# A perceiver block on one core: attention weights scaled by the product that turns them, and a context layer norm's scale and bias on GpSimd

## The chip, the cores and the metric

The kernel runs on one core of a Trainium2 chip. The metric is the device time of one execution in microseconds; the number given is the median of several runs. A profile of one execution comes with it. Engines are named as the profile names them: PE is TensorE (PEld its loads of the stationary operand), DVE is VectorE, ACT is ScalarE, POOL is GpSimd, SP is SyncE, which issues most DMAs.

## The reference, cut to what matters

64 sequences of 32 tokens of width 256 attend to contexts of 257 rows each. Two layers follow each other; each adds a cross attention, a self attention and a feed-forward part to the tokens. The two cross attentions are what the change touches.

```python
# layer 0: keys and values from the normed context and the tokens themselves
xn = layernorm(ctx, ln_x_g, ln_x_b)          # (x - m) / sqrt(v + eps) * g + b
ln = layernorm(latents, ln_l_g, ln_l_b)
q = ln @ Wq
kv = concatenate([xn @ Wkv, ln @ Wkv])       # 257 + 32 keys, 16 heads of 64
sim = einsum(rmsnorm(q) * scale, rmsnorm(k)) # masked
out = softmax(sim) @ v;  out @ Wout + bout
...
# layer 1: keys and values from the raw context, 257 keys, 16 heads of 64
scores = (q / 8) . k;  out = softmax(scores) @ v;  out @ wo + bo
```

The other parts are a self attention with 16 heads of 16, a mixture of 64 experts (8 per token, capacity 128) with a shared expert, a causal self attention in a latent space, and a linear part with tanh.

## The kernel before, in words

All arithmetic is in float32. The 2048 tokens are 16 tiles of 128 rows, each four sequences (`NB` = 4, `b` is the place in the tile). The program has three stages: `before` (layer 0 up to the routing), `experts`, and `after` (layer 1). PE's instruction order is written by hand: the whole program stands in a manual schedule for PE. The other engines' orders come from a planner, which also decides whether a copy written as `nc.any.tensor_copy` runs on DVE or ACT; `urgent()` raises the priority of what is issued inside it.

`before` loops over the 64 sequences with `CrossFirst`. One pass `s` does, in PE's order: `keys(s+2)` (16 products that make the keys of 16 heads, copies to kT at L1230 and L1232, squares at L1235), `weigh(s)`, `norms(s+2)` (L1247, sums of those squares), `values(s)` (L232, L242), `spread(s+2)` (L1268), `turn(s+3)` (L1202, contexts transposed), `scores(s+2)` (L1287, then masking and softmax), and `prepare(s+4)` (layer norm of a context, on DVE and ACT alone). Between these, `slot()` issues a piece of the tile work of the tokens: queries of the next tile, the output projection, self attention, routing. The routing ends in a scatter by eight indirect DMAs that POOL issues per tile (L665).

Scores lie with queries (4 heads x 32 tokens, four groups `g`) on the partitions and keys along the row. `softmax_rows` takes the maximum (L193), exponentials with sums (L195), a reciprocal (L198), and then scales the rows by the reciprocal: two groups on DVE (L208), two on ACT (L206). The last 33 columns are also written scaled to a second place in the tile (`twice`, L201), which the product with the tail of the values needs. `weigh` transposes the scaled weights, three chunks of 128 keys times four groups, against an identity (`keyed`, L218), and copies them to `at` (L219). `prepare` (L1183 on) subtracts the mean and multiplies by g (L1189), then multiplies by the reciprocal deviation and adds b (L1190), on DVE for each half of 128 rows; the result `cx` is what `turn` transposes and `values` reads.

`after` does the same for layer 1 with `CrossSecond`, with raw contexts and no key matrix: pass `s` is `weigh(s)`, `scores(s+2)`, `values(s)` with slots between. Its scaling is at L1393 on DVE for all four groups, its transpositions at L1405 (the third chunk repeats the last key's column over 128 columns, by a broadcast), its copies at L1406.

A product of the program, `product` (L178), is one `nc.tensor.matmul` per pair of operands: `lhsT` is the stationary operand, `rhs` the moving one. In the profile's rows the moving operand is named first after the arrow: psT<-c,sim is a transposition with sim stationary and the identity (a slice of the constants c) moving.

Of the kernel before, what the change touches and what calls it, by code (L numbers as in the profile page):

```python
# [10 lines left out]
F32 = mybir.dt.float32  # L11
# [3 lines left out]
ALU = mybir.AluOpType  # L15
AX = mybir.AxisListType

P = 128
D = 256
S = 32  # L20
NB = P // S
J = 257
JK = J + S
# [76 lines left out]
class Kernel:  # L100
    def __init__(self, ctx, tc, a, out):
        self.ctx, self.tc, self.nc, self.a, self.out = ctx, tc, tc.nc, a, out
        self.nt = out.shape[0] // P
        self.nb = self.nt * NB
        self.const = ctx.enter_context(tc.tile_pool(name="const", bufs=1))
        self.ps = ctx.enter_context(tc.tile_pool(name="ps", bufs=8, space=bass.MemoryType.PSUM))
        self.small = ctx.enter_context(tc.tile_pool(name="small", bufs=4))
# [76 lines left out]
        nc.vector.tensor_tensor(xt, xt, ps, ALU.add)  # L184


    def softmax_rows(self, sim, n, twice=None):


        nc = self.nc  # L190
        mx = self.small.tile([P, 4], F32, name="mx")
        sm = self.small.tile([P, 4], F32, name="sm")
        nc.vector.tensor_reduce(mx, sim, AX.X, ALU.max, negate=True)  # L193
        for g in range(4):
            nc.scalar.activation(  # L195
                sim[:, g, :], sim[:, g, :], AF.Exp, bias=mx[:, g : g + 1], accum_out=sm[:, g : g + 1]
            )
        nc.vector.reciprocal(sm, sm)  # L198
        if twice is not None:
            m = twice.shape[2]  # L200
            nc.vector.tensor_tensor(  # L201
                twice, sim[:, :, n - m :], sm.unsqueeze(2).to_broadcast([P, 4, m]), ALU.mult
            )
        for g in range(4):
            if g % 2:
                nc.scalar.mul(sim[:, g, :], sim[:, g, :], sm[:, g : g + 1])  # L206
            else:
                nc.vector.tensor_scalar(sim[:, g, :], sim[:, g, :], sm[:, g : g + 1], None, ALU.mult)  # L208

    def keyed(self, sim, sizes):  # L210

        nc = self.nc
        at = self.atp.tile([P, len(sizes), 512], F32, name="at")
        k0 = 0
        for j, n in enumerate(sizes):
            ps = self.bank("psT")
            for g in range(4):
                nc.tensor.transpose(ps[:n, g * P : (g + 1) * P], sim[:, g, k0 : k0 + n], self.ident)  # L218
            nc.any.tensor_copy(at[:n, j, :], ps[:n, :])  # L219
            k0 += n  # L220
        return [at[:n, j, :] for j, n in enumerate(sizes)]
# [454 lines left out]
    def experts(self, ctx, slot, tails):  # L676
# [75 lines left out]
        for e in range(AHEAD):  # L752
            weigh(e)
# [17 lines left out]
        for e in range(E):  # L771
            weigh(e + AHEAD)
            fetch(e + 3)
            turn(e + 2)
            while (at - total + rest) * E < rest * e:
                next(side)
                at += 1
            inner(e + 1)
            outer(e)
            if e == AHEAD:  # L780
                self.after_weights()
            if e == 2 * AHEAD:
                self.ffnw = self.ffn_weights(self.w2)
# [319 lines left out]
class CrossFirst:  # L1103


    def __init__(self, k, kp):
        self.k, self.kp = k, kp
        self.own, self.held, self.cx, self.xT = {}, {}, {}, {}

    def given(self, wq, wk, gx, bx, gl, bl, gam, xl, xlT):  # L1110
        self.wq, self.wk_ = wq, wk
# [71 lines left out]
    def prepare(self, s):  # L1183

        k, nc, cx = self.k, self.k.nc, self.cx[s]
        mv, rs = k.stats(cx, 2)
        for j in range(2):
            x = cx[:, j, :]
            nc.vector.scalar_tensor_tensor(x, x, mv[:, j, 0:1], self.gx, ALU.subtract, ALU.mult)  # L1189
            nc.vector.scalar_tensor_tensor(x, x, rs[:, j : j + 1], self.bx, ALU.mult, ALU.add)  # L1190

    def turn(self, s):

# [78 lines left out]
    def scores(self, s):  # L1272
        k = self.k
        nc = k.nc
        t, b = divmod(s, NB)
        _, _, qT, mb = self.own[t]
        _, _, kT, whole = self.held[s]
        sim = whole[:, :, :JK]
        for half in range(2):
            ps = [k.bank("psB") for _ in range(2)]  # L1280
            for u in range(2):
                for i in range(2):
                    for odd in range(2):
                        m = 2 * (2 * half + i) + u
                        q = PLACES[i].index(2 * u + odd)
                        r = slice(DH * odd, DH * odd + DH)
                        nc.tensor.matmul(  # L1287
                            ps[i][q * S : (q + 1) * S, :JK],
                            lhsT=qT[r, m, b * S : (b + 1) * S],
                            rhs=kT[r, m, :],  # L1290
                            start=True,
                            stop=True,
                        )
            for i in range(2):
                g = 2 * half + i
                with k.urgent():
                    nc.vector.tensor_tensor(sim[:, g, :], ps[i][:, :JK], sim[:, g, :], ALU.mult)  # L1297
        nc.vector.tensor_tensor(sim, sim, mb[:, b, :].unsqueeze(1).to_broadcast([P, 4, JK]), ALU.add)
        k.softmax_rows(sim, JK, whole[:, :, 2 * P + 64 : 2 * P + 64 + S + 1])

    def weigh(self, s):

        k = self.k
        cx, c3, _, sim = self.held.pop(s)
        at = k.keyed(sim, [P, P, P])
        self.weights = at[:2], [cx[:, 0, :], cx[:, 1, :]], (at[2], c3)

    def values(self, s):
# [7 lines left out]
class CrossSecond:  # L1316
# [54 lines left out]
    def scores(self, s):  # L1371

        k, nc = self.k, self.k.nc
        t, b = divmod(s, NB)
        cx, xT = self.cx[s]
        qk = self.qk[t]
        sim = self.kp.tile([P, 4, J], F32, name="sim")
        mx = k.small.tile([P, 4], F32, name="mx")
        sm = k.small.tile([P, 4], F32, name="sm")
        for g in range(4):  # L1380
            ps = k.bank("psY")
            k.product(
                ps[:, :J],
                [qk[:, c, b, g * P : (g + 1) * P] for c in range(2)],
                [xT[:, c, :] for c in range(2)],
            )
            nc.vector.tensor_reduce(mx[:, g : g + 1], ps[:, :J], AX.X, ALU.max, negate=True)  # L1387
            nc.scalar.activation(  # L1388
                sim[:, g, :], ps[:, :J], AF.Exp, bias=mx[:, g : g + 1], accum_out=sm[:, g : g + 1]
            )  # L1390
        nc.vector.reciprocal(sm, sm)
        for g in range(4):
            nc.vector.tensor_scalar(sim[:, g, :], sim[:, g, :], sm[:, g : g + 1], None, ALU.mult)  # L1393
        self.held[s] = sim

    def weigh(self, s):

        k, nc = self.k, self.k.nc
        sim = self.held.pop(s)
        at = self.kp.tile([P, 3, 512], F32, name="at", bufs=1)  # L1400
        for j in range(3):
            ps = k.bank("psT")
            for g in range(4):
                x = sim[:, g, j * P : (j + 1) * P] if j < 2 else sim[:, g, J - 1 :].to_broadcast([P, P])
                nc.tensor.transpose(ps[:, g * P : (g + 1) * P], x, k.ident)  # L1405
            nc.any.tensor_copy(at[:, j, :], ps)  # L1406
        self.at = at

# [93 lines left out]
```

## Time and profile before

| what | value |
|---|---|
| median of 3 runs | 2816.75 us (2816.62 to 2820.55) |
| the profiled execution's own time | 2814.6 us |
| its span | 2812.4 us |
| granted TensorE clock, mean | 0.985 |
| busy: PE, DVE, ACT, POOL | 2650.2, 1730.6, 1227.6, 542.3 us |
| transpositions of weights: L218, L1405 | 768 and 768 |
| scalings of weights: L208, L206, L1393 | 128, 128, 256 |
| context layer norm: L1189, L1190 | 128, 128 |

A row of the groups names line, engine, operation, output and inputs, shapes and count, then busy time with the mean of one instruction, then the idle time of the engine ahead of it and who ended it. A row of the timeline gives start, duration, and a run of like instructions with their count; the durations of PE overlap, so a run's pace is read from the starts. A wait's row gives who waited for whom, the total, the number of waits and the longest.

### The profile page before, as it was taken

How to read it: one execution, taken by the hardware profiler on the slowest of the kernel's cores; microseconds unless marked ns; L12 is line 12 of the kernel's file. 1: busy time of each engine (PE TensorE's matmuls, PEld its weight loads, DVE VectorE, ACT ScalarE, POOL GpSimd, SP SyncE). 2: the span in 40 equal slices, each digit the busy share in tenths (PEclk: the TensorE clock that was granted, in tenths of full speed). 3: DMA queues.
4: the chain of work that ended last, by engine and by line, in shares of the span. 5: the costliest groups of instructions: out<-in, count | busy, mean ns of one | idle time of the engine just before them, and what ended most of it. 6: DMA issues, size and time to landing. Idle time of an engine off the chain costs nothing. (4 is left out here: it accounts for less than half of the span.)

```text
span 2812.4 us, 59421 instructions
## 1 busy us (share of the span) xinstructions
PE 2650.2 (94%) x23642; PEld 1823.7 (65%) x23642; DVE 1730.6 (62%) x4544; ACT 1227.6 (44%) x3463; POOL 542.3 (19%) x644
## 2 busy tenths in 40 slices
PE   6999999999999999999998799899999999999995
PEld 4566656665666566656665578677777777777763
DVE  6565656665666567656755433556666666666664
ACT  4555555555555555555553233333333333333331
POOL 3110122112211221122112200421222222121001
PEclk9999999999999999999998799999999999999997
DMA  7000011101100000000002587221212222221110
GB/s 263 27 16 14 18 31 33 31 18 31 32 30 18 27 26 22 18 19 19 17 5 82 182 268 229 80 71 48 61 48 58 52 55 59 50 57 47 33 33 7
DMA packets 136089, 157.05 MB, mean 56 GB/s; under 512 B 24025, under 2 KB 118980, under 8 KB 135813
## 3 DMA queue, kind: packets, MB, share of 16 engines
q1 hardware_dynamic: 114308, 119.65, 14.0%
q0 software_dynamic: 12288, 25.21, 3.4%
q10 hardware_dynamic: 9216, 8.39, 0.9%
q8 instruction: 187, 3.06, 0.5%
q14 instruction: 90, 0.73, 0.1%
HBM read 121.63 MB, written 37.75 MB: 57 GB/s over the span
## 5 line engine op out<-in xcount | busy, mean ns | idle before, releaser
L178 PE MATMUL psA<-xT,wk 128*128 128x289 f32 x2048 | 522.0, 410 | 17.9 <-issue 13.0
L178 PEld LDWEIGHTS psA<-xT,wk 128*128 128x128 f32 x2048 | 384.0, 190 | 150.1 <-issue 46.5
L802 POOL DMA_INDIRECT y<-oute,idx x128 | 131.5, 1027 | 657.4 <-DVE x L813 466.8
L232 PE MATMUL psY<-at,cx 128*128 128x512 f32 x512 | 238.1, 608 | 0.0
L178 PE MATMUL psA<-at,cx 128*128 128x512 f32 x512 | 233.5, 599 | 0.0
L178 PE MATMUL psY<-xT,qk 128*128 128x257 f32 x1024 | 233.5, 380 | 0.0
L178 PEld LDWEIGHTS psY<-xT,qk 128*128 128x128 f32 x1024 | 189.8, 190 | 25.1
L1388 ACT ACTIVATE sim<-psY,mx 128x257 f32<-128x257 f32 x256 | 120.8, 476 | 148.6 <-DVE mx L1387 147.7
L232 PEld LDWEIGHTS psY<-at,cx 128*128 128x128 f32 x512 | 92.8, 191 | 123.1 <-issue 99.7
L195 ACT ACTIVATE sim<-sim,mx 128x289 f32<-128x289 f32 x256 | 135.5, 532 | 64.4 <-DVE mx L193 64.3
L178 PEld LDWEIGHTS psA<-at,cx 128*128 128x128 f32 x512 | 93.4, 190 | 96.5 <-issue 83.3
L1235 ACT ACTIVATE sq<-kT 128x1156 f32<-128x1156 f32 x128 | 148.6, 1161 | 12.6 <-DVE kT L1232 11.4
L244 ACT COPY yT<-psY 128x512 f32<-128x512 f32 x128 | 68.7, 589 | 189.8 <-PE psY L242 189.8
L1297 DVE TENSOR_TENSOR sim<-psB,sim 128x289 f32<-128x289 f32 x256 | 100.7, 451 | 81.5 <-PE psA L178 37.9
L1230 ACT COPY kT<-psA 128x289 f32<-128x289 f32 x256 | 99.2, 388 | 115.7 <-PE psA L178 113.6
L665 POOL DMA_INDIRECT buf<-z,fi x128 | 126.4, 987 | 96.3 <-DVE fi L662 54.0
L1232 DVE COPY kT<-psA 128x289 f32<-128x289 f32 x256 | 114.3, 451 | 40.0 <-PE psA L178 39.9
L178 PE MATMUL psY<-yT,wv 128*64 128x128 f32 x2048 | 127.9, 277 | 7.3 <-DVE yT L1418 7.3
L1387 DVE TENSOR_REDUCE mx<-psY 128x1 f32<-128x257 f32 x256 | 101.0, 418 | 52.6 <-PE psY L178 47.5
L178 PEld LDWEIGHTS psY<-yT,wv 128*64 128x64 f32 x2048 | 116.6, 138 | 16.3 <-DVE yT L1418 11.2
L184 DVE TENSOR_TENSOR x<-x,psY 128x256 f32<-128x256 f32 (+1 forms) x80 | 29.2, 365 | 156.4 <-PE psY L178 154.8
L178 PE MATMUL psY<-wo,oT 128*128 128x128 f32 (+1 forms) x768 | 124.2, 315 | 0.0
(254 smaller groups left out, 5005.7 us busy)
## 6 DMA issues: line engine op xcount, KB each, us to landing
cx<-in_ctx SPq DMA_DIRECT2D x128, 256.0 KB
we<-in_m_ew SPq DMA_DIRECT2D x64, 384.0 KB
xT<-in_ctxT SPq DMA_DIRECT2D x64, 257.0 KB
buf<-zero SPq DMA_DIRECT2D x32, 256.0 KB
be<-buf SPq DMA_DIRECT2D x64, 128.0 KB
oute<-oe ACTq DMA_DIRECT2D x64, 128.0 KB
mu<-in_mask SPq DMA_DIRECT2D x16, 128.5 KB
x<-in_x SPq DMA_DIRECT2D x16, 128.0 KB
```

Source lines behind the costliest of these rows:

```text
L178: self.nc.tensor.matmul(ps, lhsT=lhs[i], rhs=rhs[i], start=(i == 0), stop=(i == n - 1))
L195: nc.scalar.activation(sim[:, g, :], sim[:, g, :], AF.Exp, bias=mx[:, g : g + 1], accum_out=sm[:, g : g + 1])
L232: nc.tensor.matmul(ps[kc], lhsT=values[i][:, kc * P : (kc + 1) * P], rhs=at[i], start=(i == 0), stop=(i == n - 1 and tail is None),)
L244: nc.any.tensor_copy(yT[:, kc, :, b * S : (b + 1) * S], ps[kc].rearrange("p (h i) -> p h i", h=H))
L665: d = nc.gpsimd.indirect_dma_start(out=self.buf[:, :], out_offset=bass.IndirectOffsetOnAxis(ap=fi[:, k : k + 1], axis=0), in_=z[:, 0, :], ...
L802: nc.gpsimd.indirect_dma_start(out=y, out_offset=None, in_=self.oute[:, :], in_offset=bass.IndirectOffsetOnAxis(ap=self.idx[:, t, k : k + ...
L1230: nc.scalar.copy(kT[:, p, :], ps[:, :JK])
L1232: nc.vector.tensor_copy(kT[:, p, :], ps[:, :JK])
L1235: nc.scalar.activation(sq[p // 4], kT[:, p - 3 : p + 1, :], AF.Square)
L1297: nc.vector.tensor_tensor(sim[:, g, :], ps[i][:, :JK], sim[:, g, :], ALU.mult)
L1387: nc.vector.tensor_reduce(mx[:, g : g + 1], ps[:, :J], AX.X, ALU.max, negate=True)
L1388: nc.scalar.activation(sim[:, g, :], ps[:, :J], AF.Exp, bias=mx[:, g : g + 1], accum_out=sm[:, g : g + 1])
```

## The change

The rows of the weights are no longer scaled. `diagonal` makes, for each group, the identity with the reciprocal sums on its diagonal (`dg`, one DVE operation for all four groups), and `turned` multiplies the unscaled weights with it instead of transposing them against the identity: the product transposes and scales at once. The copy of the last 33 columns to their second place is now unscaled and runs on GpSimd. The contexts' layer norm in `prepare` is done by `layernorm` (subtract and multiply by the reciprocal deviation, L152, on DVE), and its scale g and bias b follow on GpSimd as two operations over both halves.

```diff
-    def softmax_rows(self, sim, n, twice=None):
+    def softmax_rows(self, pool, sim, n, twice=None):
...
+        if twice is not None:
+            nc.gpsimd.tensor_copy(twice, sim[:, :, n - twice.shape[2] :])
+        return self.diagonal(pool, sm)
+
+    def diagonal(self, pool, sm):
+
+        nc = self.nc
         nc.vector.reciprocal(sm, sm)
-        if twice is not None:
-            m = twice.shape[2]
-            nc.vector.tensor_tensor(
-                twice, sim[:, :, n - m :], sm.unsqueeze(2).to_broadcast([P, 4, m]), ALU.mult
-            )
-        for g in range(4):
-            if g % 2:
-                nc.scalar.mul(sim[:, g, :], sim[:, g, :], sm[:, g : g + 1])
-            else:
-                nc.vector.tensor_scalar(sim[:, g, :], sim[:, g, :], sm[:, g : g + 1], None, ALU.mult)
+        dg = pool.tile([P, 4, P], F32, name="dg", bufs=2)
+        nc.vector.tensor_tensor(
+            dg, self.ident.unsqueeze(1).to_broadcast([P, 4, P]), sm.unsqueeze(2).to_broadcast([P, 4, P]), ALU.mult
+        )
+        return dg
+
+    def turned(self, ps, x, dg):
+
+        self.nc.tensor.matmul(ps, lhsT=x, rhs=dg, start=True, stop=True)
...
-                nc.tensor.transpose(ps[:n, g * P : (g + 1) * P], sim[:, g, k0 : k0 + n], self.ident)
+                self.turned(ps[:n, g * P : (g + 1) * P], sim[:, g, k0 : k0 + n], dg[:, g, :])
...
     def prepare(self, s):
 
         k, nc, cx = self.k, self.k.nc, self.cx[s]
-        mv, rs = k.stats(cx, 2)
-        for j in range(2):
-            x = cx[:, j, :]
-            nc.vector.scalar_tensor_tensor(x, x, mv[:, j, 0:1], self.gx, ALU.subtract, ALU.mult)
-            nc.vector.scalar_tensor_tensor(x, x, rs[:, j : j + 1], self.bx, ALU.mult, ALU.add)
+        k.layernorm(cx, cx)
+        nc.gpsimd.tensor_tensor(cx, cx, self.gx.unsqueeze(1).to_broadcast([P, 2, D]), ALU.mult)
+        nc.gpsimd.tensor_tensor(cx, cx, self.bx.unsqueeze(1).to_broadcast([P, 2, D]), ALU.add)
...
-        k.softmax_rows(sim, JK, whole[:, :, 2 * P + 64 : 2 * P + 64 + S + 1])
+        dg = k.softmax_rows(self.kp, sim, JK, whole[:, :, 2 * P + 64 : 2 * P + 64 + S + 1])
+        self.ready[s] = dg
...
-        nc.vector.reciprocal(sm, sm)
-        for g in range(4):
-            nc.vector.tensor_scalar(sim[:, g, :], sim[:, g, :], sm[:, g : g + 1], None, ALU.mult)
-        self.held[s] = sim
+        self.held[s] = sim, k.diagonal(self.kp, sm)
...
-                nc.tensor.transpose(ps[:, g * P : (g + 1) * P], x, k.ident)
+                k.turned(ps[:, g * P : (g + 1) * P], x, dg[:, g, :])
```

In the kernel after the change these lines lie at L199 (copy on GpSimd), L207 (dg), L214 (the turning product, in both stages), L225 and L1408 (copies to `at`), L1193 and L1194 (scale and bias on GpSimd).

More of the change, by code (lines that the diff above doesn't have):

```diff
@@ L197, in softmax_rows, with keyed @@
             )
-        nc.vector.reciprocal(sm, sm)
-        if twice is not None:
-            m = twice.shape[2]
-            nc.vector.tensor_tensor(
-                twice, sim[:, :, n - m :], sm.unsqueeze(2).to_broadcast([P, 4, m]), ALU.mult
-            )
-        for g in range(4):
-            if g % 2:
-                nc.scalar.mul(sim[:, g, :], sim[:, g, :], sm[:, g : g + 1])
-            else:
-                nc.vector.tensor_scalar(sim[:, g, :], sim[:, g, :], sm[:, g : g + 1], None, ALU.mult)
-    def keyed(self, sim, sizes):
+        if twice is not None:
[3 more added lines that the diff above has]
+        nc = self.nc
+        nc.vector.reciprocal(sm, sm)
+        dg = pool.tile([P, 4, P], F32, name="dg", bufs=2)
[5 more added lines that the diff above has]
+        self.nc.tensor.matmul(ps, lhsT=x, rhs=dg, start=True, stop=True)
+    def keyed(self, sim, dg, sizes):
         nc = self.nc
@@ L1107, in __init__ @@
         self.k, self.kp = k, kp
-        self.own, self.held, self.cx, self.xT = {}, {}, {}, {}
+        self.own, self.held, self.cx, self.xT, self.ready = {}, {}, {}, {}, {}
     def given(self, wq, wk, gx, bx, gl, bl, gam, xl, xlT):
@@ L1304, in weigh @@
         cx, c3, _, sim = self.held.pop(s)
-        at = k.keyed(sim, [P, P, P])
+        at = k.keyed(sim, self.ready.pop(s), [P, P, P])
         self.weights = at[:2], [cx[:, 0, :], cx[:, 1, :]], (at[2], c3)
@@ L1390, in scores @@
             )
-        nc.vector.reciprocal(sm, sm)
-        for g in range(4):
-            nc.vector.tensor_scalar(sim[:, g, :], sim[:, g, :], sm[:, g : g + 1], None, ALU.mult)
-        self.held[s] = sim
+        self.held[s] = sim, k.diagonal(self.kp, sm)
     def weigh(self, s):
         k, nc = self.k, self.k.nc
-        sim = self.held.pop(s)
+        sim, dg = self.held.pop(s)
         at = self.kp.tile([P, 3, 512], F32, name="at", bufs=1)
```

## The prediction

> **What bounds the kernel now.** I read the page's first two parts first: who is busy, and whether that holds in every stage.
>
> ```profile
> PE 2650.2 (94%) x23642; PEld 1823.7 (65%) x23642; DVE 1730.6 (62%) x4544; ACT 1227.6 (44%) x3463; POOL 542.3 (19%) x644
> ...
> PE   6999999999999999999998799899999999999995
> PEclk9999999999999999999998799999999999999997
> ```
>
> TensorE is busy 94% of the span and shows a 9 in nearly every slice, at the full granted clock; no other engine passes two thirds. A busy PE need not be PE at its limit, so I asked for the two stretches of attention (first: 64 sequences by the loop with `turn`, `keys`, `weigh`; second: 64 sequences with `CrossSecond`). Columns: length, then busy time and count of PE, PEld, DVE, ACT, POOL, granted clock, DMA.
>
> ```profile
> 60.00:1450.00 1390.00, 1347.19 (x11379) 855.22 (x11377) 893.99 (x2483) 746.75 (x2058) 272.46 (x358) 1.00 0.09 25
> 1930.00:2780.00 850.00, 818.32 (x8320) 608.97 (x8319) 554.56 (x1271) 289.98 (x862) 160.26 (x154) 1.00 0.18 49
> ```
>
> PE lacks 42.8 us of 1390 in the first and 31.7 of 850 in the second. So every microsecond added to PE's own stream there is added to the end, except where it falls into one of these gaps; and a microsecond taken from DVE or ACT buys nothing unless it shortens one. Which gaps those are is told by the waits of PE in the first stretch:
>
> ```profile
> PE psA L178 <- issue: 12.1, 28, 1.0
> PE psB L1247 <- ACT sq L1235: 10.3, 14, 2.0
> PE psB L1287 <- ACT qTf L1167: 6.7, 15, 1.8
> ```
>
> In the loop's order `norms` (L1247) comes after `weigh`, so its 10.3 us (14 waits, mean 0.74) is time that a longer `weigh` covers. L1287 waits for a copy of transposes that were issued after `weigh`; it isn't covered. The second stretch's largest wait, 14.0 us for zT (L162), lies between a transposition and its own product, nowhere near `weigh`.
>
> **The change, part 1: what a turned tile costs on PE.** The 12 transpositions of a sequence become 12 products with a scaled diagonal. The group rows say that one record of either takes the same: 275 and 273 ns (transpositions, L1405 and L218) against 278 (psA<-zT,wq, an ordinary product of the same shape). That is the time through the pipeline, not the pitch. The pitch comes from the timeline (start, duration, count), where the next row's start closes each burst:
>
> ```profile
> 2016.27 3.84 PE L178 MATMUL psA<-zT,wq 128*128 128x128 f32 x32 [0.73 <-ACT zT L162]
> 2019.95 1.47 PE L1405 MATMUL psT<-c,sim 128*128 128x128 f32 x12
> 2021.26 1.03 PE L178 MATMUL psY<-xT,qk 128*128 128x257 f32 x4
> ...
> 1651.61 1.06 PE L178 MATMUL psA<-beT,we 128*128 128x128 f32 x8
> 1652.50 0.60 PE L178 MATMUL psY<-we,eact 128*128 128x256 f32 x2
> ```
>
> The transpositions: (2021.26 - 2019.95)/12 = 109 ns each. The products: (2019.95 - 2016.27)/32 = 115 ns and (1652.50 - 1651.61)/8 = 111 ns a record. And the count is what matters: `queries` writes 16 products for zT,wq and the trace has 32 records; `inner` writes 4 and it has 8; `weigh` writes 12 transpositions and it has 12. An f32 product is two records, a transposition is one. A turned tile therefore goes from 109 ns to between 2 x 111 = 222 and 2 x 115 = 230 ns: 113 to 121 more. There are 768 in each stretch, 1536 in all: 1536 x 0.113 = 174 us to 1536 x 0.121 = 186 us. I take 1536 x 0.118 = 181 us, a little nearer the bigger row, because mixed streams (psY<-wo,oT, 116 to 118 ns in the timeline) sit there. Per sequence that is 1.41 us.
>
> A rule speaks here. The Trainium skill, "TensorE: Matmul & The Clock Gate", section Terms, says that the transposition mode is four times faster for FP32. By it a product would cost 4 x 109 = 436 ns and the change 1536 x 0.327 = 502 us, a time near 3319. The rows above contradict that as a pitch: products with 128 columns stand at 222 to 230. The same page, section LDWEIGHTS, has a load of the stationary operand last columns/1.2 ns, 107 for 128: both kinds load 128 columns per record, and that floor hides most of the fourfold. I go by the rows.
>
> **Part 2: what leaves DVE and ACT.** DVE loses the scaling of weights (256 of L1393 at 364 ns, 128 of L208 at 377, 64 of L201 at 295: 160 us) and of contexts (128 of L1189 at 476, 128 of L1190 at 544: 131 us); it gains 128 diagonals (128x512 with two inputs; nearest row L309, 683 ns: 87 us) and 128 passes of normalising (two per context; L152, 256 columns, 0.44 us: 56 us). ACT loses 128 of L206 at 536 ns (69 us). The planner that places `any` copies answers by moving copies of `at`: in the built order DVE has 63 of 384 where it had 212, so 149 x 0.68 = 101 us more leave DVE and 149 x 0.59 = 88 us come to ACT. Sum: DVE about -249, ACT about +19. On the path this is worth only what it takes from PE's waits: nothing beyond the L1247 row, which part 1 covers too. I count it once: -10 us.
>
> The new wait: `weigh` now waits for the diagonal. Behind it in PE's queue stand `norms`, `values`, `spread` and all that follows. In the timeline a sequence's last L208 ends at 664.3 and its `weigh` starts at 683.6, 19 us later; a 0.68 us diagonal in place of two scalings comes no later. Zero; without that cover it would be 0.7 x 128 = 87 us.
>
> **Part 3: what comes to GpSimd.** Two operations of 128x512 for each of 64 contexts. Bounds for one: twice L1123 (128x256, 774 ns) gives 1.5 us, twice L1122 (919) gives 1.8, L1011 (128x512, strided input) 1.53. I take 1.5: 128 x 1.5 = 192 us, and 64 copies of 4x33 at some 0.4 us (L1206, 64 elements, 0.31): 26 us. POOL goes from 542 to 760 us. No DMA moves with it, but POOL's queue carries the scatter of routed rows (8 DMA issues at 1.28 us pitch after a 4.3 us wait, some 15 us per tile) and the mask (L1174, 3.64 us). In the built order a context's two operations stand ahead of the scatter that could hold them, and the copy into the tail of the weights follows the scatter only where its `weigh` is over a sequence away. The tightest place that I find: DVE ends a context at 705.9, PE turns the next at 719.1; 3 us more of POOL fit into 13. Zero, with the bound of a full miss in the rivals. At the start POOL gets three contexts' operations, 9 us, between 18 and 35 us, before q (L1151 ended at 31.7, read by PE at 33.1): about +1 us, once.
>
> **Sum.** Against the profiled execution's own 2814.6 us (span 2812.4): 2814.6 + 181 - 10 + 1 = 2986.6. The median of the runs is 2.2 above that execution: 2988.8, rounded to 2988.
>
> **Rivals.**
> 1. *PE's gaps swallow more.* 74.5 us of gaps stand in both stretches. If the lighter DVE also closes half of them (37 us instead of 10), 2961. Against it: the unnamed waits ("issue", 12.1 us) come once per tile wherever the scatter runs, and zT's lie elsewhere.
> 2. *GpSimd becomes the bound in the first stretch.* If contexts come late behind a scatter once per tile, 12 tiles x up to 10 us add 120: 3108; if both operations lay wholly on PE's path, 60 x 3 = 180: 3168. For it: POOL is strictly in order and holds long waits; against it: the margins of 13 us and more, and 34% use after the change (470 of 1390).
> 3. *The other side: the turning product costs no more than the transposition.* Place: L214's pitch. If the diagonal product is a single record (112 against 109 ns: 1536 x 3 ns = +5 us) while ACT's relief removes the 10 us of L1247 and a few of the rest, the time is 2817 + 5 - 12 = 2810, faster. It decides below 109 + 12/1.536 = 117 ns per tile. Against it: every f32 product in the trace has two records.
> 4. *The fourfold rule holds after all*: 3319.
>
> **How the numbers follow.** My forecast, products as record pairs and no new stall: 0.80, alone within 2970 to 3005 (174 to 186 us, with nothing or 20 us swallowed). Rival 1: 0.06; rival 2: 0.09; rival 3: 0.03; rival 4: 0.02. The range 2962 to 3015 reaches to rival 1's time and to the small end of rival 2. A measurement of this kernel tells 0.2% (5.6 us) from no change. Faster 0.03, same 0.01 (a pitch near rival 3's limit), slower 0.96.
>
> **What would show it.** Right: L214 has 1536 records in each stretch and a burst of 24 takes about 2.7 us where 12 took 1.31; the first stretch's period grows by about 1.3 us per sequence and the second's by 1.4; L1251's wait for sq is gone; DVE falls to about 1480 us, POOL rises to about 760; PE's share rises to 95%. Wrong: 12 records per burst (rival 3); a PE wait at the transposition of contexts for POOL cx L1194, or at L214 for POOL L199 or DVE dg (rival 2); a burst of 5 us (rival 4).

## The result, and the profile after

The kernel after takes 2968.62 us (median of 4, 2966.16 to 2970.87) where the kernel before takes 2816.78: ratio 1.0535, 95% interval 1.0515 to 1.0556, or +152 us. The forecast was 2988 (+171), the range 2962 to 3015. The direction and the price of the product hold; the size is 19 us off, and the parts of that are below.

The page of the kernel after, first part (busy time, share, instructions), then two of its groups on PE (line, operation, names, shapes, count; busy, mean ns; idle before):

```profile
PE 2823.4 (95%) x25178; PEld 2007.2 (68%) x25178; DVE 1576.8 (53%) x3970; ACT 1275.0 (43%) x3461; POOL 741.5 (25%) x836
...
L214 PE MATMUL psT<-dg,sim 128*128 128x128 f32 x3072 | 367.8, 276 | 2.6 <-issue 2.4
L1251 PE MATMUL psB<-sq,c 128*32 128x289 f32 x1024 | 78.9, 413 | 1.2 <-ACT sq L1239 1.0
```

PE's count has risen by 25178 - 23642 = 1536: each of the 1536 turned tiles is now two records instead of one. The mean of one record is 276 ns where the transpositions had 275 and 273, so the mean tells nothing of the price. The timeline (start, duration, run) does:

```profile
2105.46 3.84 PE L178 MATMUL psA<-zT,wq 128*128 128x128 f32 x32 [0.73 <-ACT zT L162]
2109.13 2.84 PE L214 MATMUL psT<-dg,sim 128*128 128x128 f32 x24
2111.81 3.64 PE L178 MATMUL psY<-xT,qk 128*128 128x257 f32 x16
```

The 24 records hold PE for 2111.81 - 2109.13 = 2.68 us, 111.7 ns each (PE is held from a record's start to the next record's start). The same place took 1.31 us for 12 transpositions: +1.37 us per sequence.

Where in the program the time came from is read from the starts of four bursts of turned tiles: the first, the 64th (end of the first stretch), the 65th and the 128th. First the kernel before, then the kernel after:

```profile
61.99 1.47 PE L218 MATMUL psT<-c,sim 128*128 128x128 f32 x12
...
1512.38 1.47 PE L218 MATMUL psT<-c,sim 128*128 128x128 f32 x12
...
1800.32 2.77 PE L1405 MATMUL psT<-c,sim 128*128 128x128 f32 x12
...
2745.74 1.47 PE L1405 MATMUL psT<-c,sim 128*128 128x128 f32 x12
```

```profile
64.55 2.84 PE L214 MATMUL psT<-dg,sim 128*128 128x128 f32 x24
...
1581.57 2.84 PE L214 MATMUL psT<-dg,sim 128*128 128x128 f32 x24
...
1868.14 5.01 PE L214 MATMUL psT<-dg,sim 128*128 128x128 f32 x24
...
2900.73 2.84 PE L214 MATMUL psT<-dg,sim 128*128 128x128 f32 x24
```

| stage, us | before | after | difference |
|---|---|---|---|
| start to first burst | 62.0 | 64.5 | +2.6 |
| first to 64th (63 sequences) | 1450.4 | 1517.0 | +66.6 |
| 64th to 65th (rest of the first part, experts) | 287.9 | 286.6 | -1.3 |
| 65th to 128th (63 sequences) | 945.4 | 1032.6 | +87.2 |
| 128th to the end | 66.6 | 66.2 | -0.4 |

The 65th bursts take 2.77 and 5.01 us because the granted clock was 0.50 and 0.53 there, after PE had stood for some 6 us.

In the second stretch the price of the product arrives whole: 63 x 1.37 = 86 of 87 us. In the first stretch 20 us of it are missing. Adding up, for each PE group there, the time from each record's start to the next one's: the turned tiles go from 89.9 to 174.8 us (+84.9); norms (psB<-sq) from 91.0 to 71.3 (-19.7); scores (psB<-kT,qTf) from 83.3 to 92.6 (+9.3); keys and the transpositions of z lose 5.9, and what is left of the stretch 2. The norms' gain is seen in one place of the timeline, once per tile. Before, then after:

```profile
664.17 0.68 PE L1247 MATMUL psB<-sq,c 128*32 128x289 f32 x4
665.39 1.17 PE L1247 MATMUL psB<-sq,c 128*32 128x289 f32 x12 [0.54 <-ACT sq L1235]
```

```profile
690.50 1.18 PE L1251 MATMUL psB<-sq,c 128*32 128x289 f32 x16
```

Before, PE did four norms, then stood until ACT had the second half of the squares; after, all sixteen run through. `weigh` stands ahead in PE's queue and has grown by 1.37 us. But the squares came sooner, too. Their second half at these two places, before and after:

```profile
664.19 1.15 ACT L1235 ACTIVATE sq<-kT 128x1156 f32<-128x1156 f32 x1
```

```profile
687.51 1.17 ACT L1239 ACTIVATE sq<-kT 128x1156 f32<-128x1156 f32 x1
```

Counted from the start of `weigh` (661.05 and 686.01), the squares were complete after 4.3 us before and after 2.7 us now; the norms began after 3.1 us before and after 4.5 us now. Either move alone would have been enough to end the wait here. Eleven tiles have this place, and it makes 14.5 of the 19.7 us (the other long norms stand at the start of the stretch); on the mean over them the squares went from 4.4 to 2.4 us. So this pair does not show which of the two took the wait away.

### The profile page after: what moved, and what is told of

Its sections match the earlier page's. It is cut to its first block, busy times and chain, and to the rows that moved or that the text cites. A ratio compares the mean times of both kernels' runs of the same rounds, so it can differ in the third digit from the quotient of the medians.

```text
span 2966.9 us, 62129 instructions
## 1 busy us (share of the span) xinstructions
PE 2823.4 (95%) x25178; PEld 2007.2 (68%) x25178; DVE 1576.8 (53%) x3970; ACT 1275.0 (43%) x3461; POOL 741.5 (25%) x836
## 4 chain that ended last, share of the span: by engine, by line
PE 86%; DVE 6%; ACT 4%; issue 2%; DMA 2%; POOL 0%; SPq 0%; POOLq 0%; DVEq 0%; ACTq 0%
PE psA L178 34%; PE psY L178 18%; PE psT L214 12%; PE psY L238 8%; PE psB L1251 2%; PE psY L248 2%; PE psB L1291 2%; PE psA L1353 1%; PE psY L328 1%; PE psB L178 1%; PE psT L161 1%; PE psR L1272 1%; DMA cx<-in_ctx 1%; DVE st L141 1%; ACT sim L1273 1%
## 5 line engine op out<-in xcount | busy, mean ns | idle before, releaser
L178 PE MATMUL psA<-xT,wk 128*128 128x289 f32 x2048 | 526.0, 414 | 11.3 <-issue 5.3
L178 PEld LDWEIGHTS psA<-xT,wk 128*128 128x128 f32 x2048 | 389.4, 193 | 141.8 <-issue 29.5
L214 PEld LDWEIGHTS psT<-dg,sim 128*128 128x128 f32 x3072 | 363.4, 193 | 12.9 <-issue 4.3
L214 PE MATMUL psT<-dg,sim 128*128 128x128 f32 x3072 | 367.8, 276 | 2.6 <-issue 2.4
L178 PE MATMUL psA<-at,cx 128*128 128x512 f32 x512 | 233.3, 598 | 0.0
L178 PE MATMUL psY<-xT,qk 128*128 128x257 f32 x1024 | 232.9, 380 | 0.0
L178 PEld LDWEIGHTS psY<-xT,qk 128*128 128x128 f32 x1024 | 189.3, 190 | 24.9
L1408 ACT COPY at<-psT 128x512 f32<-128x512 f32 x191 | 110.4, 585 | 176.0 <-PE psT L214 118.6
L1193 POOL TENSOR_TENSOR cx<-cx,a_gx 128x512 f32<-128x512 f32 x64 | 87.9, 1373 | 368.5 <-DVE cx L152 357.5
L178 PEld LDWEIGHTS psA<-at,cx 128*128 128x128 f32 x512 | 93.4, 190 | 96.5 <-issue 74.4
```

The lines of the kernel that those rows point to most:

```text
L178: self.nc.tensor.matmul(ps, lhsT=lhs[i], rhs=rhs[i], start=(i == 0), stop=(i == n - 1))
L214: self.nc.tensor.matmul(ps, lhsT=x, rhs=dg, start=True, stop=True)
```

## Experiments

All ran on chips 1, 5 and 13, where the kernel before takes 2751 to 2754 us, not 2817. The record names no chip for the pair above; that it was another one is inferred from the time, and "the first chip" below means the one of that pair. Each experiment is compared with the kernel before on its own chip, and the expectations given as absolute times are read as differences. In which part of the program the times differ is told with the two unchanged kernels below.

**The product alone.** The kernel before, with transpositions issued as products with the identity:

```diff
...
-                nc.tensor.transpose(ps[:n, g * P : (g + 1) * P], sim[:, g, k0 : k0 + n], self.ident)
+                nc.tensor.matmul(ps[:n, g * P : (g + 1) * P], lhsT=sim[:, g, k0 : k0 + n], rhs=self.ident, start=True, stop=True)
...
-                nc.tensor.transpose(ps[:, g * P : (g + 1) * P], x, k.ident)
+                nc.tensor.matmul(ps[:, g * P : (g + 1) * P], lhsT=x, rhs=k.ident, start=True, stop=True)
```

> The kernel before with its 12 transpositions per sequence issued as ordinary f32 products against the identity; every scaling on DVE and ACT stays. Theory (the longer weigh covers the wait of norms for the squares): 1536 x (2 x 111.5 - 109) ns = +175 us, less some 18 us of waits covered, 2974 us (2966 to 2982), and the wait of L1247 for ACT falls below 2 us. Rival (the lighter DVE and ACT took that wait away): the wait stays near 10 us and the time is 2990 us or more.

Measured 2926.54 against 2751.31: ratio 1.0631 (1.0611 to 1.0652), +175 us. So the whole loss is there without any diagonal, any scaling moved or any GpSimd work: it is the price of an f32 product against a transposition. (The planner answered this edit as well: DVE makes 111 of the 384 copies to `at` here, 212 in the kernel before and 63 in the kernel after.) The theory's time (+157) is missed, although the wait of L1247 fell to 1.9 us as it said, for two reasons that the stages show against the unchanged kernel's profile: these chips have little wait at the norms to cover (next experiments), and the last stage is 8.3 us longer here (74.5 against 66.2). PE has two unnamed stops there, 2.6 and 1.8 us, and the granted clock of that stage is 0.73 against 0.78:

```profile
PE psY L322 <- issue: 2.6, 1, 2.6
...
PE psB L1050 <- issue: 1.8, 1, 1.8
```

The two stretches alone grew by 78.7 and 82.5 us.

**The relief alone.** The kernel after with the products put back to transpositions against the identity:

```diff
     def turned(self, ps, x, dg):

-        self.nc.tensor.matmul(ps, lhsT=x, rhs=dg, start=True, stop=True)
+        self.nc.tensor.transpose(ps, x, self.ident)
```

> The kernel after with the 12 products per sequence put back to transpositions against the identity; dg is still made but not used, so the division of the attention weights by their sums is left out. Theory: without the longer weigh the wait for the squares is back (8 us or more in L1251), 2810 to 2818 us, so the relief of DVE and ACT is worth next to nothing. Rival: the relief alone takes the wait away, 2798 us or less.

Measured 2759.46 (2754.18 to 2766.93) against 2751.31: ratio 1.003 (1.0013 to 1.0046). As differences the theory had -7 to +1 us and the rival -19: measured +8, past the theory's end and away from the rival. DVE's and ACT's lighter load buys nothing here. The profiled execution was the fastest (2754.18), so where the rest of the 8 us lies is not seen. The norms hold PE for 75.6 us in the first stretch, as in the unchanged kernel (75.3); with the product alone it is 69.6. So on these chips the longer `weigh` took what wait there was, and the lighter ACT did not. That is 6 us, nearly all of it near the start of the stretch. It does not carry over to the first pair, whose waits stand mostly elsewhere.

**The contexts' scale and bias alone.** The kernel before with the new `prepare`:

```diff
-        mv, rs = k.stats(cx, 2)
-        for j in range(2):
-            x = cx[:, j, :]
-            nc.vector.scalar_tensor_tensor(x, x, mv[:, j, 0:1], self.gx, ALU.subtract, ALU.mult)
-            nc.vector.scalar_tensor_tensor(x, x, rs[:, j : j + 1], self.bx, ALU.mult, ALU.add)
+        k.layernorm(cx, cx)
+        nc.gpsimd.tensor_tensor(cx, cx, self.gx.unsqueeze(1).to_broadcast([P, 2, D]), ALU.mult)
+        nc.gpsimd.tensor_tensor(cx, cx, self.bx.unsqueeze(1).to_broadcast([P, 2, D]), ALU.add)
```

> The kernel before with only the contexts' scale and bias moved to GpSimd. Theory: hidden, within 4 us of the kernel before (2816 to 2821), the start some 2 us later. Rival: GpSimd's extra work beside the scatter is what lengthens the scores (kT,qTf) by 9 us in the kernel after, then 2824 to 2828.

Measured 2764.09 against 2751.31: ratio 1.0047 (1.003 to 1.0064), +12.8 us. Theory missed, and the rival's place too: the scores hold PE as long as before (73.3 against 73.6 us). Against the unchanged kernel's profile the start is 3.0 us longer, the first stretch 7.4 and the last stage 4.5. The waits of PE name two causes:

```profile
PE psB L1245 <- ACT sq L1233: 10.6, 7, 3.4
...
PE psA L178 <- POOL cx L1187: 3.3, 1, 3.3
```

The second is the start: the first context now ends on GpSimd, and the first keys wait for it. The first goes with the planner's new order: the squares come later, and the norms hold PE 7.5 us longer (82.8). In the kernel after on these chips the norms hold PE for 71.5 us, so next to nothing of this is left there.

**The turned products without the move to GpSimd.** The kernel after with the old `prepare` (the previous diff, undone):

> The kernel after with the contexts' layer norm back on DVE as before. Theory: 2966 us (2962 to 2972), the start 2 us earlier. Rival (the move to GpSimd costs some 12 us, at the start and beside the scatter): 2957 us.

Measured 2917.69 against 2751.31: ratio 1.0598 (1.0576 to 1.062), +166 us. As differences the theory had +149 and the rival +140, both drawn from the first pair; what tells them apart here is the kernel after on these chips (next), some 2 us above it as differences and 3.7 as times, where the theory had 3 and the rival 12. So in the kernel after the move to GpSimd costs 2 to 4 us in all, not 12. The wait for cx at the start is gone. The start itself (61.9 us to the first burst) proves little: the unchanged kernel before has 62.0 us in one profile and 64.9 in another, at granted clocks of 1.00 and 0.84 between 45 and 66 us.

**Both kernels unchanged, on these chips.**

> The kernel before, unchanged, for its profile on this chip. Chips differ: where the four experiments so far ran, the kernel before took 2751 us. Theory: there PE's unnamed stops beside the scatter are missing, and the first stretch alone (first to 64th weigh) is some 50 us shorter than the 1450 us of the profile before; the second stretch is the same 945 us. Rival: all stages are shorter in one proportion (2%), so 1419 and 925 us.

> The kernel after, unchanged, on the same chip as its parts. Theory (parts add up): products alone +175, lighter DVE and ACT alone some +8 with the start's +3 in it, so 2751 + 166 to 2751 + 178; the start is 3 us later than in the kernel before for the contexts on GpSimd. Rival: the parts help each other and the whole is below +160.

The kernel before: 2753.99 against 2753.33. In the order of the table above its stages are 64.9, 1389.3, 284.1, 947.6 and 66.2 us. The first stretch is 61 us shorter than in the profile of the prediction and the second 2 longer: the theory's picture, the rival's proportion is out. The timeline beside the scatter shows what is missing. First the profile of the prediction, then this chip:

```profile
648.76 1.20 PE L1287 MATMUL psB<-kT,qTf 64*32 64x289 f32 x30
650.29 0.64 PE L1287 MATMUL psB<-kT,qTf 64*32 64x289 f32 x2 [0.33 <-issue]
650.87 0.44 PE L161 MATMUL psT<-c,z 128*128 128x128 f32 x2
651.74 1.25 PE L178 MATMUL psA<-xT,wk 128*128 128x289 f32 x3 [0.43 <-issue]
653.20 1.10 PE L178 MATMUL psA<-xT,wk 128*128 128x289 f32 x3 [0.21 <-issue]
654.61 6.60 PE L178 MATMUL psA<-xT,wk 128*128 128x289 f32 x26 [0.30 <-issue]
```

```profile
637.91 1.20 PE L1287 MATMUL psB<-kT,qTf 64*32 64x289 f32 x32
639.05 0.44 PE L161 MATMUL psT<-c,z 128*128 128x128 f32 x2
639.32 7.97 PE L178 MATMUL psA<-xT,wk 128*128 128x289 f32 x32
```

The same program, the same place: there PE stops every few records, here it runs through, and from the first of the scores to the end of the keys it takes 3.1 us less (12.3 us to 661.05, 9.2 to 647.13). DVE stands there as well: its first operation on these scores, first chip and this chip:

```profile
654.66 1.56 DVE L1297 TENSOR_TENSOR sim<-psB,sim 128x289 f32<-128x289 f32 x4 [4.25 <-PE psA L178]
```

```profile
639.48 1.54 DVE L1297 TENSOR_TENSOR sim<-psB,sim 128x289 f32<-128x289 f32 x4
```

In each of twelve tiles it starts 3.7 to 4.8 us after PE's last score there; here it follows in 0.2 us as a rule. ACT is held up with it: its copy of zT waits 4.0 us, to 654.94. The squares come later as well (4.3 us after the start of `weigh`, here 3.0), and so the norms wait in this tile, 2.32 us against 1.11. One tile of four sequences lasts 94.3 us there and 90.0 here (from scatter to scatter): the 4.3 us are 3.1 of stops and 1.2 of that wait.

The kernel after: 2921.36 against 2753.33, ratio 1.0609 (1.0581 to 1.0637), +168 us, inside the theory's +166 to +178. Its stretches grew by 80.2 and 84.5 us over the unchanged kernel's profile here; the norms give 3.8 us, not 19.7. This is what makes +168 here of +152 there: the first stretch grows by 13.6 us more here, and the norms' part of that is 15.9. Most of the wait that the kernel after no longer had on the first chip stood right behind the stops, and where they are missing it is missing, too. What the stops cost outside the norms stays nearly the same (45 us in the kernel before, 48 in the kernel after: the first stretch without its norms, there less here).

**One record instead of two.** The kernel after with the old `prepare`, weights and diagonal in float32r:

```diff
...
-        dg = pool.tile([P, 4, P], F32, name="dg", bufs=2)
+        dg = pool.tile([P, 4, P], F32R, name="dg", bufs=2)
...
-        self.sim = [w.tile([P, 4, 3 * P], F32, name=f"sim{i}") for i in range(3)]
+        self.sim = [w.tile([P, 4, 3 * P], F32R, name=f"sim{i}") for i in range(3)]
...
-        sim = self.kp.tile([P, 4, J], F32, name="sim")
+        sim = self.kp.tile([P, 4, J], F32R, name="sim")
```

> The kernel after with the contexts' layer norm back on DVE, and the 12 products in float32r instead of float32 (weights and diagonal written in that type). Theory: the price of the product is its two records; a float32r product is one record at some 112 ns, so the 1536 products cost 1536 x 3 ns = 5 us more than transpositions, and with the lighter DVE and ACT the time is within 12 us of the kernel before on the same chip. Rival: pace is set by something else than records (the type, reading dg), and the time stays over 100 us above.

Measured 2750.84 (20 runs) against 2753.33: ratio 0.999 (0.9983 to 0.9997). Its neighbour in float32 (the turned products without the move to GpSimd) had +166 us; they are gone. What set the price was the second record. The group and one burst:

```profile
L215 PE MATMUL psT<-dg,sim 128*128 128x128 f32 x1536 | 209.6, 286 | 0.0
```

```profile
1865.96 1.64 PE L215 MATMUL psT<-dg,sim 128*128 128x128 f32 x12
1867.43 3.69 PE L179 MATMUL psY<-xT,qk 128*128 128x257 f32 x16
```

1536 records again. From the starts this burst has 1.47/12 = 122 ns a tile, but that is not the pace: within the bursts the records follow each other at 112 ns (median of the intervals after the first), where the transpositions had 109. The first record starts early, 26 to 29 ns behind the record ahead of it in four bursts looked at, and then 245 to 276 ns pass to the second. This is why the tiles hold PE 96.2 us in the first stretch against 84.1, and the keys ahead of them 13 us less, which evens out. This is the one version faster than both kernels, by 0.1% (2.5 us, on the edge of what can be told); what the type costs in precision was not measured here.

**The same in the second stretch only**, the first as in the kernel before:

```diff
...
-        sim = self.kp.tile([P, 4, J], F32, name="sim")
+        sim = self.kp.tile([P, 4, J], F32R, name="sim")
...
-        for g in range(4):
-            nc.vector.tensor_scalar(sim[:, g, :], sim[:, g, :], sm[:, g : g + 1], None, ALU.mult)
-        self.held[s] = sim
+        dg = self.kp.tile([P, 4, P], F32R, name="dg", bufs=2)
+        nc.vector.tensor_tensor(
+            dg, k.ident.unsqueeze(1).to_broadcast([P, 4, P]), sm.unsqueeze(2).to_broadcast([P, 4, P]), ALU.mult
+        )
+        self.held[s] = sim, dg
...
-                nc.tensor.transpose(ps[:, g * P : (g + 1) * P], x, k.ident)
+                nc.tensor.matmul(ps[:, g * P : (g + 1) * P], lhsT=x, rhs=dg[:, g, :], start=True, stop=True)
```

> The kernel before, with the products by the diagonal in float32r in the second stage alone; the first stage keeps its transpositions and scalings. Theory: 768 x 3 ns = 2 us more on PE, DVE lighter by some 40 us where it isn't waited for: within 5 us of the kernel before. Rival: some 88 us more, as for float32 products.

Measured 2763.13 against 2753.33: ratio 1.0034 (1.0021 to 1.0046), +9.8 us, outside the 5 expected, and far from the rival's 88. The stretch itself is 948.8 us against 947.6; 8.7 us are in the last stage, 74.9 against 66.2, with the same two stops as in the product alone (2.3 us at L323, 1.5 at L1051) and a granted clock of 0.71 there. Both places are streams of 32x32 products with a hundred and more short records; why some builds stop there is open.

**Without the scatter**, the kernel before and the kernel after:

```diff
-        for k in range(TOPK):
-            d = nc.gpsimd.indirect_dma_start(
-                out=self.buf[:, :],
...
-            self.tc.add_to_no_dep_group("scatter", d.ins)
```

> The kernel before without the routed rows' scatter (the eight indirect DMAs per tile are left out, so the experts get zeros). In the profiles of the prediction PE stops for 2 to 3 us per tile while the scatter runs; on the chips of the later runs it doesn't. Theory, on a chip with the stops (kernel before at 2817): the scatter causes them, and without it the time falls by 50 us or more to some 2755. On a chip without them (kernel before at 2751 to 2754): within 5 us of the kernel before. Rival, on a chip with the stops: the time stays above 2800.

> The kernel after without the same scatter (experts get zeros). Theory, on a chip with the stops (kernel after at 2969): it falls to some 2921, the time of the kernel after where there are none, so that the change costs 165 to 172 us without the stops on either chip. On a chip without them: within 5 us of the kernel after (2921). Rival: stops stay, and the difference of the two kernels without the scatter stays 152 us.

The chip was again one without the stops. 2744.86 against 2752.87 (ratio 0.9964, 0.9946 to 0.9983) and 2915.39 (ratio 1.0573, 1.0511 to 1.0636): the first is 8 us below the kernel with it, the second 6 us below the kernel after on the chip of the previous runs, both a little more than the 5 allowed. The change costs 170.5 us without the scatter. Whether the scatter causes the stops on the first chip stays open: neither kernel ran there without it.

## Why the prediction was right

*Two records against one* (part 1): right, and shown three ways: by the count of 3072, by the product alone (+175), and by the return of the time with a one-record product. The price was put at 118 ns more per tile; it is 2 x 111.7 - 109 = 114, the lower end given, so 175 us instead of 181. The choice "nearer the bigger row" was wrong by 6 us: the bursts of psA<-zT,wq and psY<-wo,oT that drew it up begin with one interval of 213 ns and go on at 111 to 112.

*The rule of a fourfold transposition*: the rows decided rightly; the measured ratio is 223/109 = 2.05. That the load of the stationary operand is the floor was argued, not shown; one group in the trace before fits it: records with the same 128 moving columns but 64 stationary ones (psY<-yT,wv) follow each other at 57 ns, not 112.

*The covered waits* (the -10 in the sum): right that the wait at L1247 goes, mis-sized, and open in its cause. The waits' row for L1247 counts only time in which PE is seen idle. The time that the norms held PE was 91.0 us for 62 groups that take 1.11 us undisturbed, so 22 us could be had, and 19.7 were. The term should have been twice as large. 14.5 us of it stood behind the stops, where the longer `weigh` and the earlier squares would each have been enough, and on chips without the stops the term is 3.8 us. There the two errors nearly cancel (175 - 4 against 181 - 10), so that +168 lies so close to the forecast of +171 is in part luck.

*Terms not foreseen*: scores hold PE 9.3 us longer in the first pair, keys and z 5.9 less. The unnamed stops beside the scatter now fall at another place of PE's stream: in the waits they go from L178 (12.1 to 5.3 us) to L1291 (3.1 to 5.8) and L161 (3.9 to 5.8). On chips without the stops the scores stay at 73.4 to 73.6. The first stretch's period grew by 66.6/63 = 1.06 us per sequence, not by the 1.3 forecast.

*The start* (+1): PE waits 2.6 us for cx (L1193), because the first context's operations end on GpSimd; the step that named q as the late one had the wrong tile. That the start is 2.6 us longer in all decides nothing: two profiles of the kernel before differ there by 2.9.

*DVE*: the durations of the operations that the forecast names fell by 239 us, forecast 249 (the normalising takes 533 ns, not 440). All durations on DVE fell by 220, and busy time by only 154, because it counts overlapping instructions once; so DVE came to 1577 us, not to the 1480 given as a sign. POOL rose by 199 of 218 forecast. On the chips without stops both are off the path: "nothing beyond the L1247 row" is what the relief alone showed there.

*Small slips in the sums*: 0.7 x 128 is 90 us, not 87, and 2988.8 rounds to 2989. Nothing hangs on either.

*The rivals*: rival 1 (more of PE's gaps swallowed, 2961) comes within 8 us of the result where the forecast is 19 off. What was swallowed beyond the forecast lies at the norms; whether DVE's and ACT's lighter load had a part in it is not settled for the first chip. Rival 2: of its kind is only the single wait for cx at the start, 2.3 to 3.3 us in the kernels with the move; the +12.8 us of the move alone lie mostly at the norms and in the last stage. Rival 3 (one record per product, then no loss) is what the float32r version does, 2.5 us below the kernel before; for float32 it is out.

## What to carry to other kernels

A transposition of 128x128 by an identity is one record on PE here and an f32 product of the same shape is two, so folding a scaling into the transposition doubles its price (1.31 to 2.68 us per sequence); with PE as the bound, the relief of DVE and ACT did not pay it back. Read the pace of PE from the starts of a burst and the number of records per written product, not from the mean of one. What a longer step may cover is the time by which the next group is stretched, not the idle time that its row names. When a wait goes away, look at both sides of it: here the waiting step came later and what it waited for came sooner.

## What the runs showed of the hardware that was not expected

The same program took 2816.8 us in the pair and 2751 to 2754 on chips 1, 5 and 13, 2.3% less, nearly all of it in the first stretch (61 us). Beside the scatter PE stops there and DVE and ACT are held up with it, 3.1 us of a tile's 94.3 us, and the norms wait 1.2 us behind that. The change costs 152 us where the stops are and 168 where they are not. Their cause is open. A float32r product of 128x128 runs as one record at a pace of 112 ns, where a float32 one takes two, 223 ns.
